# One tile for each PSUM bank in a four-layer graph network, with two-bank tiles for the ranked phases only

## The chip, the cores and the metric

The kernel runs on one core of a Trainium2 chip. The metric is the device time of one execution in microseconds; the time before is the median of three runs, 771.85 us (771.4 to 771.99). The profiled execution of the same kernel took 771.36 us, and its profile covers a span of 769.6 us, from the first to the last instruction of the program. All instants below are microseconds from the start of that span.

## What is computed

The input is a feature matrix x of 3327 nodes by 64 features and a weighted, sparse adjacency matrix of 3327 by 3327 in float32. Four graph layers follow each other, each as a residual after a layer normalisation and a ReLU:

```python
h = relu(layernorm(x));  x = x + L0(h, adj)   # two gated cells, each with its own adj product
h = relu(layernorm(x));  x = x + L1(h, adj)   # weights from the rank of each nonzero in its row
h = relu(layernorm(x));  x = x + L2(h, adj)   # three hops with w = adj * adj
h = relu(layernorm(x));  x = x + L3(h, adj)   # two hops with tanh

# L0, one cell
m  = adj @ (x @ W)
gi = m @ wih.T + bih;  gh = x @ whh.T + bhh
r  = sigmoid(i_r + h_r);  z = sigmoid(i_z + h_z)
n  = tanh(i_n + r * h_n)
out = (1 - z) * n + z * x

# L1
mask = adj != 0;  rank = cumsum(mask, axis=1);  deg = rank[:, -1:]
k = minimum(deg, 100);  pos = rank - (deg - k)
out = (mask * where(pos > 0, 0.5 ** (k - pos), 0)) @ (h @ weight) + bias
```

So eight products with a matrix of the size of adj are formed, numbered k = 0 to 7 in the kernel: 0, 1 (gated cells), 2 (ranked), 3, 4, 5 (squared), 6, 7 (plain). Everything else is small beside them.

## The kernel before

The nodes are padded to two halves of 13 blocks of 128. The result columns are split into four chunks (three of 3 blocks, one of 4), and the chunks into two groups, (0, 1) and (2, 3). A tile of adj holds 128 source nodes and the columns of one group; it is loaded from HBM into one of 19 slots on chip. For each product k and each chunk, 26 tiles are accumulated into one PSUM bank (`sums`); then the chunk's follow-up work begins. The follow-up work is a Python generator: each `yield us` says after how many microseconds of accumulating matmuls its next piece is written into the instruction streams. The engines run their own streams in order; what is written early on an engine is carried out early there.

```python
CH = [(0, 3), (3, 6), (6, 9), (9, 13)]
GROUPS = [(0, 1), (2, 3)]
STREAM_US = 0.86
...
    pairs = [psum.tile([P, 2, CWM], F32, name=f"bank{i}") for i in range(4)]
    idle_sums, idle_temps = deque(range(4)), deque(range(4, 8))
    counting = []

    def bank(i):
        return pairs[i // 2][:, i % 2]

    def take(sums=False):
        pool = idle_sums if sums or counting else idle_temps
        for c in list(tasks):
            if not pool and c not in running:
                advance(c)
        i = pool.popleft()
        return i, bank(i)

    def give(i):
        (idle_sums if i < 4 else idle_temps).append(i)
```

All eight banks are thus held as four tiles of two banks each. `take` hands out one bank, and it can lie in the same tile as another bank that is in use. Banks 0 to 3 are for the long accumulations, 4 to 7 for small products. In the ranked product (k = 2) banks 4 to 7 are used as two pairs: a running count of nonzeros is kept by matmuls with two constant matrices (`tri`, `rest`) and read by one ScalarE instruction over both banks of a pair. While `counting` holds, small products take their banks from 0 to 3.

```python
    def expand(k, c, t):                       # ranked and squared tiles
        ...
        if not counting:
            while len(idle_temps) < 4:
                advance(next(iter(tasks)))
            counting.append(True)
        a, b = GROUPS[t.g]
        pair = pairs[2 if c == a else 3]
        for s in range(2):
            if t.before is not None:
                mm(pair[:, s, :w], rest, t.before.view[:, s, t.cols(c)], start=False, unchecked=True)
            mm(pair[:, s, :w], tri, t.mask.view[:, s, t.cols(c)], start=t.before is None, unchecked=True)
        spend(STREAM_US * w / CWM)
        nc.scalar.activation(wide, pair[:, :, :w], AF.Relu, bias=bitsb, scale=-TWO7)       # L353
        ...

    def propagate(k, c, t, rhs, first, last):  # the accumulating matmuls
        ...
                nc.tensor.matmul(acc[h * D:(h + 1) * D, :w], yq, rhs[:, h, :], ...)         # L376
        ...
        spend(STREAM_US * w / CWM * (0.75 if KIND[k] == RANKED else 1.0))
        if last:
            begin(c, after[k](c, sums.pop((k, c))))

    def evacuate(acc, c):
        m = work.tile([P, CWM], F32, name="t2")[:, :width(c)]
        if c % 2:
            nc.scalar.copy(m, acc[1][:, :width(c)])                                        # L452
        else:
            nc.vector.tensor_copy(m, acc[1][:, :width(c)])                                 # L454
        give(acc[0])
        return m

    def gru(acc, c, hT, ih, hh, bi, bh, cell):
        w = width(c)
        m = evacuate(acc, c)
        yield 0.8
        ...
        for g, gate in enumerate((r, z)):
            i, ps = take()
            mm(ps[:, :w], bd[:, hh + g, :], hT, stop=False)                                # all small products: L179
            mm(ps[:, :w], bd[:, ih + g, :], m, start=False)
            nc.scalar.activation(gate, ps[:, :w], AF.Sigmoid, bias=bsum[:, cell, g:g + 1]) # L525
            give(i)
        pn = take(), take()
        for (_, ps), wt, ft in zip(pn, (hh + 2, ih + 2), (hT, m)):
            mm(ps[:, :w], bd[:, wt, :], ft)
        yield 1.0
        nc.vector.scalar_tensor_tensor(t, pn[0][1][:, :w], bcol[...], r, op0=ALU.add, op1=ALU.mult)  # L533
        nc.vector.tensor_tensor(t, t, pn[1][1][:, :w], ALU.add)                            # L534
        for i, _ in pn:
            give(i)
        nc.scalar.activation(n, t, AF.Tanh, bias=bcol[:, bi + 2:bi + 3])                   # L537
        yield 1.3
        ...                                                                                # L539 to L543: hT of the cell

    def after_hop(k):                          # the hops have the same beginning, with dense_to_nodes
        def done(c, acc):
            m = evacuate(acc, c)
            yield 0.8
            v = dense_to_nodes([(m, WL2 + k - 3)], c)
            ...
```

The order of the work: `alone` runs one product for one group, `joint` two products of one group side by side, so that each loaded tile serves both; in the last tiles of a group the order is swept chunk by chunk, so that chunk a of the group ends some tiles before chunk b.

Of the kernel before, what the change touches and what calls it, by code (L numbers as in the profile page):

```python
# [9 lines left out]
F32 = mybir.dt.float32  # L10
# [29 lines left out]
P = 128  # L40
# [6 lines left out]
CWM = 512  # L47
# [33 lines left out]
def kernel(  # L81
# [14 lines left out]
    psum = ctx.enter_context(tc.tile_pool(name="psum", bufs=1, space=bass.MemoryType.PSUM))  # L96
# [73 lines left out]
    def width(c):  # L170
        return blocks(c) * P

    def mm(out, lhsT, rhs, start=True, stop=True, unchecked=False):

        for h in range(2):
            hs = slice(h * D, (h + 1) * D)
            nc.tensor.matmul(out[hs], lhsT[:, hs], rhs, start=start, stop=stop, skip_group_check=unchecked)  # L179

    pairs = [psum.tile([P, 2, CWM], F32, name=f"bank{i}") for i in range(4)]
    idle_sums, idle_temps = deque(range(4)), deque(range(4, 8))
    counting = []

    def bank(i):
        return pairs[i // 2][:, i % 2]

    def take(sums=False):  # L190

# [9 lines that stand above are left out]
# [5 lines left out]
    def features(c):  # L206
        return feat.tile([P, width(c)], F32, name=f"hT{c}")
# [17 lines left out]
    def advance(c):  # L225
        running.add(c)
        try:
            tasks[c][1] = next(tasks[c][0])
        except StopIteration:
            del tasks[c]  # L230
        running.discard(c)
# [6 lines left out]
    def finish(c):  # L238
        while c in tasks:
            advance(c)  # L240

    def spend(us):

        for c in list(tasks):
            if c in tasks and c not in running:
                tasks[c][1] -= us
                if tasks[c][1] <= 0:
                    advance(c)
# [57 lines left out]
    def square(sq, v, turn):  # L306
        if turn % 3:
            nc.scalar.activation(sq, v, AF.Square)  # L308
        else:
            nc.vector.tensor_tensor(sq, v, v, ALU.mult)  # L310
# [16 lines left out]
    def expand(k, c, t):  # L327

        w = width(c)
        if KIND[k] == PLAIN or t.in_place:  # L330
            return t.view(c)
        wide = work.tile([P, 2, CWM], I16 if KIND[k] == RANKED else F32, name="w4", bufs=4)[:, :, :w]
        if KIND[k] == SQUARED:
            square(wide, t.view(c), t.q + c)
            return wide

        if not counting:
            while len(idle_temps) < 4:
                advance(next(iter(tasks)))
            counting.append(True)
        a, b = GROUPS[t.g]
        pair = pairs[2 if c == a else 3]
        for s in range(2):
            if t.before is not None:
                mm(pair[:, s, :w], rest, t.before.view[:, s, t.cols(c)], start=False, unchecked=True)  # L350
# [3 lines that stand above are left out]
        if c == b:  # L354
            if t.before is not None:
                t.before.free()
            if t.q == 0:
                t.mask.free()
                if t.g == 1:
                    counting.clear()  # L360
        return wide.bitcast(BF16)

    def propagate(k, c, t, rhs, first, last):
# [72 lines left out]
    def run():  # L436
        count = {}
        prepared, expanded = 0, deque()
        for i, (k, c, t) in enumerate(units):
            while prepared < len(units) and prepared < i + PREPARE[KIND[units[prepared][0]]]:  # L440
                prepare(*units[prepared])
                prepared += 1
            while len(expanded) < min(EXPAND + 1, len(units) - i):
                expanded.append(expand(*units[i + len(expanded)]))
            n = count[k, c] = count.get((k, c), 0) + 1
            propagate(k, c, t, expanded.popleft(), n == 1, n == NQ)
# [10 lines that stand above are left out]
# [57 lines left out]
# [5 lines that stand above are left out]
        rz = work.tile([P, 2, CWM], F32, name="w4", bufs=4)  # L519
        r, z = rz[:, 0, :w], rz[:, 1, :w]  # L520
        for g, gate in enumerate((r, z)):
            i, ps = take()
            mm(ps[:, :w], bd[:, hh + g, :], hT, stop=False)
# [7 lines that stand above are left out]
        nt = work.tile([P, 2, CWM], F32, name="w4", bufs=4)  # L531
        t, n = nt[:, 0, :w], nt[:, 1, :w]
        nc.vector.scalar_tensor_tensor(t, pn[0][1][:, :w], bcol[:, bh + 2:bh + 3], r, op0=ALU.add, op1=ALU.mult)  # L533
        nc.vector.tensor_tensor(t, t, pn[1][1][:, :w], ALU.add)  # L534
        for i, _ in pn:
            give(i)
        nc.scalar.activation(n, t, AF.Tanh, bias=bcol[:, bi + 2:bi + 3])  # L537
        yield 1.3
        nc.vector.tensor_tensor(r, hT, n, ALU.subtract)  # L539
        nc.vector.tensor_tensor(r, r, z, ALU.mult)  # L540
        nc.vector.tensor_tensor(r, r, n, ALU.add)
        o = features(c)
        nc.vector.tensor_scalar(o, r, 0.0, None, op0=ALU.max)  # L543
        yield 2.4
        return o
# [29 lines left out]
    def after_0(c, acc):  # L575
        hT[c] = yield from gru(acc, c, hT[c], IH1, HH1, BI1, BH1, 0)
        i, v = transpose_to_nodes(hT[c], c)
        yield 0.8
        yk = nodes(c)
        nc.vector.tensor_copy(flat(yk), v)  # L580
        give(i)
        y[1][c] = yk

    def after_1(c, acc):
        h2T = yield from gru(acc, c, hT[c], IH2, HH2, BI2, BH2, 1)
        v = transpose_to_nodes(h2T, c)
        yield 0.8
        residual(v, c)
        yk = nodes(c)
        yield from layernorm_relu(yk, c, TWO27, pace=1.5)  # L590
        add_row(c, 3)
        y[2][c] = yield from in_three(yk, c)
# [84 lines left out]
    run()  # L677
    for c in list(tasks):
        finish(c)


# [37 lines left out]
```

## Time and profile before

| what | value |
|---|---|
| median of three runs | 771.85 us |
| span of the profile | 769.6 us |
| TensorE (PE) matmuls | 721.3 us busy, 94% of the span |
| ScalarE (ACT) | 250.8 us, 33% |
| VectorE (DVE) | 235.7 us, 31% |
| adjacency tiles loaded | 286, of 768 or 896 KB, 243.55 MB with the rest of that queue |
| DMA queue of these loads | 83.3% of sixteen engines' span |
| granted TensorE clock | 1.00 throughout |

The page of the profile gives busy time and its share for each engine, the span in 40 slices, the chain of work that ended last, and groups of like instructions. The list of waits says for each engine and line how long it sat idle, and whose end released it: total, number of times, longest. PE stands for the matmuls and PEld for the weight loads that go ahead of them; one stop of the engine is listed under both. In the timeline a number in square brackets is the engine's idle time before that instruction. Where matmuls overlap in the pipeline, the profile's end of a matmul is modelled, and so "busy" is not the same as "at full rate".

### The profile page before, as it was taken

Reading aid. Unit: us, or ns where it says so; the run is one execution under the profiler, and the core shown is the slowest. Engines: PE = TensorE matmul, PEld = TensorE weight load, DVE = VectorE, ACT = ScalarE, POOL = GpSimd, SP = SyncE. Lnnn points to the kernel's source line nnn. Section 1 sums busy time; section 2 is a strip of 40 time slices with the busy share of each in tenths; the row PEclk is TensorE's granted clock in tenths of the full one; section 3 lists DMA queues with packets and bytes.
Section 4 is the critical chain, followed back from the end, with each engine's and each line's share of the span. In section 5 each row is a group of like instructions: output and inputs, shape, how many; then the busy total and the mean of one; then the engine's idle time right before and its main releaser. Section 6 shows DMA issues by size and latency. Waiting matters only on the chain.

```text
span 769.6 us, 12248 instructions
## 1 busy us (share of the span) xinstructions
PE 721.3 (94%) x5240; PEld 357.4 (46%) x5240; DVE 235.7 (31%) x346; ACT 250.8 (33%) x314; POOL 42.0 (5%) x38
## 2 busy tenths in 40 slices
PE   3977999999988999999999999999999999999997
PEld 2422433334536667776435544334344444344443
DVE  6102101215449447431944212430151510000000
ACT  1101001101036777778947421840054501000000
POOL 5000000001102001100300000000020000000000
PEclk9999999999999999999999999999999999999999
DMA  9999993669999999995999939972999199906991
GB/s 294 401 401 406 405 405 123 218 248 405 401 401 356 374 384 390 373 384 194 408 403 400 403 112 394 405 277 69 372 350 319 63 367 405 346 21 227 385 403 54
DMA packets 79174, 245.29 MB, mean 319 GB/s; under 512 B 4880, under 2 KB 5520, under 8 KB 79120
## 3 DMA queue, kind: packets, MB, share of 16 engines
q1 hardware_dynamic: 78240, 243.55, 83.3%
q10 hardware_dynamic: 880, 0.96, 0.4%
q8 instruction: 41, 0.67, 0.3%
q14 instruction: 13, 0.11, 0.0%
HBM read 243.64 MB, written 0.85 MB: 318 GB/s over the span
## 4 chain that ended last, share of the span: by engine, by line
PE 80%; DMA 9%; DVE 6%; ACT 1%; SPq 1%; issue 1%; POOL 1%; ACTq 0%; DVEq 0%; POOLq 0%
PE bank L376 64%; PE bank L179 16%; DMA adj<-in_adjT 8%; SPq L273 1%; DVE t L454 1%; DMA brow<-in_bias_rows 1%; POOL st L497 1%; ACT w L525 1%; DVE st L489 0%; DVE st L495 0%; DVE xs L505 0%; DVE t L494 0%; ACT w L353 0%; DVE y L501 0%; DVE t L491 0%
## 5 line engine op out<-in xcount | busy, mean ns | idle before, releaser
L376 PE MATMUL bank<-adj,y 128*64 128x384 f32 (+1 forms) x2704 | 492.5, 517 | 29.6 <-DMA adj<-in_adjT 19.0
L376 PEld LDWEIGHTS bank<-adj,y 128*64 128x64 f32 x2704 | 197.6, 137 | 294.5 <-issue 217.0
L353 ACT ACTIVATE w<-bank,bitsb 128x768 int16<-128x768 f32 x104 | 98.9, 953 | 31.2 <-PE bank L179 30.4
L308 ACT ACTIVATE adj<-adj 128x768 f32<-128x768 f32 (+1 forms) x103 | 85.9, 905 | 29.9 <-DMA adj<-in_adjT 25.0
L454 DVE COPY t<-bank 128x384 f32<-128x384 f32 x16 | 8.9, 557 | 280.3 <-PE bank L376 280.3
L376 PE MATMUL bank<-w,adj 128*64 128x384 bf16 (+1 forms) x624 | 73.9, 340 | 4.5 <-ACT adj L561 1.4
L179 PE MATMUL bank<-adj,tri 128*64 128x384 bf16 (+1 forms) x416 | 72.4, 339 | 0.0
L179 PE MATMUL bank<-adj,rest 128*64 128x384 bf16 (+1 forms) x400 | 70.3, 339 | 0.0
L320 DVE TENSOR_SCALAR adj<-adj 128x1536 bf16<-128x1536 f32 (+1 forms) x52 | 53.1, 1027 | 49.8 <-PE bank L179 35.9
L310 DVE TENSOR_TENSOR adj<-adj 128x768 f32<-128x768 f32 (+1 forms) x53 | 53.8, 1062 | 45.7 <-DMA adj<-in_adjT 42.4
L497 POOL TENSOR_TENSOR st<-st,mhalf 128x6 f32<-128x6 f32 (+1 forms) x16 | 27.5, 1763 | 576.8 <-DVE st L496 576.8
L525 ACT ACTIVATE w<-bank,bsum 128x384 f32<-128x384 f32 (+1 forms) x16 | 9.7, 607 | 139.0 <-PE bank L179 139.0
L376 PEld LDWEIGHTS <-adj 128*64 128x64 bf16 x624 | 40.0, 110 | 20.4 <-issue 2.3
L376 PE MATMUL bank<-w,y 128*64 128x384 f32 x208 | 36.6, 488 | 1.5 <-DVE w L310 0.8
L308 ACT ACTIVATE w<-adj 128x768 f32<-128x768 f32 x35 | 27.5, 838 | 16.8 <-PE bank L376 10.4
L452 ACT COPY t<-bank 128x384 f32<-128x384 f32 (+1 forms) x16 | 8.5, 531 | 74.1 <-PE bank L376 68.5
L179 PEld LDWEIGHTS <-tri 128*64 128x64 bf16 x416 | 26.5, 110 | 10.7 <-issue 1.2
L179 PEld LDWEIGHTS <-rest 128*64 128x64 bf16 x400 | 25.7, 110 | 9.9 <-issue 0.5
L480 ACT COPY hT<-bank 128x384 f32<-128x384 f32 (+1 forms) x12 | 6.1, 505 | 64.6 <-PE bank L179 64.6
L179 PE MATMUL bank<-bd,t 128*64 128x128 f32 (+1 forms) x320 | 26.0, 279 | 0.6 <-ACT t L452 0.4
L179 PE MATMUL bank<-hT,bd 128*64 128x384 f32 (+1 forms) x96 | 21.2, 521 | 5.7 <-ACT w L525 5.7
L310 DVE TENSOR_TENSOR w<-adj 128x768 f32<-128x768 f32 x17 | 16.0, 956 | 26.8 <-PE bank L376 20.7
(62 smaller groups left out, 263.7 us busy)
## 6 DMA issues: line engine op xcount, KB each, us to landing
adj<-in_adjT SPq DMA_DIRECT2D x156, 768.0 KB, 10.6
adj<-in_adjT SPq DMA_DIRECT2D x130, 896.0 KB, 9.6
adj<-in_weights SPq DMA_DIRECT2D x2, 352.0 KB, 7.1
xs<-in_x SPq DMA_DIRECT2D x1, 640.0 KB, 5.0
out<-xs ACTq DMA_DIRECT2D x3, 192.0 KB, 1.9
out<-xs ACTq DMA_DIRECT2D x1, 256.0 KB, 6.4
xs<-in_x SPq DMA_DIRECT2D x1, 192.0 KB, 2.4
brow<-in_bias_rows ACTq DMA_DIRECT2D x1, 96.0 KB, 6.8
```

The lines of the kernel that those rows point to most:

```text
L179: nc.tensor.matmul(out[hs], lhsT[:, hs], rhs, start=start, stop=stop, skip_group_check=unchecked)
L273: nc.sync.dma_start(out=slots[self.slot][:, :, :self.w], in_=adjT[self.q * P:(self.q + 1) * P, :].rearrange("p (s w) -> p s w", s=2)[:, :, ...
L308: nc.scalar.activation(sq, v, AF.Square)
L310: nc.vector.tensor_tensor(sq, v, v, ALU.mult)
L320: nc.vector.tensor_scalar(t.mask.view, t.view(), 0.0, None, op0=ALU.not_equal)
L353: nc.scalar.activation(wide, pair[:, :, :w], AF.Relu, bias=bitsb, scale=-TWO7)
L376: nc.tensor.matmul(acc[h * D:(h + 1) * D, :w], yq, rhs[:, h, :], start=first and n == 0, stop=last and n == len(terms) - 1)
L452: nc.scalar.copy(m, acc[1][:, :width(c)])
L454: nc.vector.tensor_copy(m, acc[1][:, :width(c)])
L480: nc.scalar.copy(ft, ps[:, :width(c)])
L497: nc.gpsimd.tensor_tensor(st[:, 3, :n], st[:, 2, :n], mhalf[:, :n], ALU.pow)
L525: nc.scalar.activation(gate, ps[:, :w], AF.Sigmoid, bias=bsum[:, cell, g:g + 1])
```

## The change

The four sum banks become four tiles of one bank. The other four banks are held in a pool of PSUM that exists twice in turn: as four tiles of one bank (`temp`), and, while the ranked product of the two groups runs, as two tiles of two banks (`pair`). `exchange` ends the one pool and opens the other at the points where the ranked product begins and ends. Its purpose is that a wait for one bank no longer covers its neighbour, while the ranked phase keeps its two-bank reads. The second part moves the writing of tanh in the gated cell: it is written one piece later, with the two `yield`s 1.0 and 0.8 in place of one of 1.3, so that ScalarE does not come to stand before tanh while its operand is still being computed. The arithmetic is the same, and so is the number of instructions that compute.

```diff
--- before.py
+++ after.py
@@ -180,12 +180,23 @@
 
 
 
-    pairs = [psum.tile([P, 2, CWM], F32, name=f"bank{i}") for i in range(4)]
     idle_sums, idle_temps = deque(range(4)), deque(range(4, 8))
+    sum_banks = [psum.tile([P, CWM], F32, name=f"sum{i}") for i in range(4)]
     counting = []
 
+    def second_half(names, shape):
+        pool = tc.tile_pool(name=names, bufs=1, space=bass.MemoryType.PSUM, reuse_waits="tile")
+        p = pool.__enter__()
+        return pool, [p.tile(shape, F32, name=f"{names}{i}") for i in range(2 if len(shape) > 2 else 4)]
+
+    half = [second_half("temp", [P, CWM])]
+
+    def exchange(names, shape):
+        half[0][0].__exit__(None, None, None)
+        half[0] = second_half(names, shape)
+
     def bank(i):
-        return pairs[i // 2][:, i % 2]
+        return sum_banks[i] if i < 4 else half[0][1][i - 4]
 
     def take(sums=False):
 
@@ -343,8 +354,9 @@
             while len(idle_temps) < 4:
                 advance(next(iter(tasks)))
             counting.append(True)
+            exchange("pair", [P, 2, CWM])
         a, b = GROUPS[t.g]
-        pair = pairs[2 if c == a else 3]
+        pair = half[0][1][c == b]
         for s in range(2):
             if t.before is not None:
                 mm(pair[:, s, :w], rest, t.before.view[:, s, t.cols(c)], start=False, unchecked=True)
@@ -358,6 +370,7 @@
                 t.mask.free()
                 if t.g == 1:
                     counting.clear()
+                    exchange("temp", [P, CWM])
         return wide.bitcast(BF16)
 
     def propagate(k, c, t, rhs, first, last):
@@ -534,8 +547,9 @@
         nc.vector.tensor_tensor(t, t, pn[1][1][:, :w], ALU.add)
         for i, _ in pn:
             give(i)
+        yield 1.0
         nc.scalar.activation(n, t, AF.Tanh, bias=bcol[:, bi + 2:bi + 3])
-        yield 1.3
+        yield 0.8
         nc.vector.tensor_tensor(r, hT, n, ALU.subtract)
         nc.vector.tensor_tensor(r, r, z, ALU.mult)
         nc.vector.tensor_tensor(r, r, n, ALU.add)
@@ -677,6 +691,7 @@
     run()
     for c in list(tasks):
         finish(c)
+    half[0][0].__exit__(None, None, None)
 
 
 # ---- launch: one core; the host only lays the arrays out ----
```

## The prediction

> **What bounds the kernel.** I read the busy times first, then the chain that ended last, then the list of waits, then the timeline around the waits. The page says that the matmul engine is the one to look at:
>
> ```profile
> PE 721.3 (94%) x5240; PEld 357.4 (46%) x5240; DVE 235.7 (31%) x346; ACT 250.8 (33%) x314; POOL 42.0 (5%) x38
> ...
> PE 80%; DMA 9%; DVE 6%; ACT 1%; SPq 1%; issue 1%; POOL 1%; ACTq 0%; DVEq 0%; POOLq 0%
> ```
>
> PE holds 80% of the chain and DMA 9%, so a stop of PE is paid in full, except in stretches where PE would only meet its next tile earlier. PE is idle for 769.6 - 721.3 = 48.3 us. The list of waits (engine and line, releaser, total us, times, longest) tells what that idle time is:
>
> ```profile
> PEld bank L376 <- DVE t L454: 18.5, 13, 2.4
> PE bank L376 <- DMA adj<-in_adjT: 19.0, 15, 12.3
> PEld bank L179 <- ACT w L525: 11.5, 8, 1.7
> PE bank L376 <- DVE t L454: 10.6, 14, 1.8
> PE bank L179 <- ACT w L525: 5.7, 8, 0.8
> ACT w L537 <- DVE w L534: 20.2, 8, 2.9
> ```
>
> The DMA line is mostly the start (12.3 us in one wait). The two lines that matter are the 14 waits of an accumulating matmul (L376) for L454, and the 8 waits of a gate matmul (L179) for L525. L454 copies a finished sum of chunk a out of its bank; the matmul that waits belongs to chunk b and writes another bank, the other half of the same two-bank tile. Nothing in the arithmetic asks for it. The timeline at one such place:
>
> ```profile
> 445.52 3.07 PE L376 MATMUL bank<-adj,y 128*64 128x384 f32 x17
> 448.62 0.56 DVE L454 COPY t<-bank 128x384 f32<-128x384 f32 x1 [5.00 <-PE bank L376]
> 449.24 1.51 PE L376 MATMUL bank<-adj,y 128*64 128x384 f32 x8 [0.65 <-DVE t L454]
> 450.58 0.82 PE L179 MATMUL bank<-bd,t 128*64 128x128 f32 x12
> ```
>
> PE ends at 448.59, DVE copies from 448.62 to 449.18, PE goes on at 449.24. The gates show the same form: z (or the pair after it) is to be written while r (or z) is being read by the sigmoid in the other half of the tile:
>
> ```profile
> 217.39 0.58 ACT L525 ACTIVATE w<-bank,bsum 128x384 f32<-128x384 f32 x1 [0.65 <-PE bank L179]
> 218.02 0.20 PEld L179 LDWEIGHTS bank<-hT,bd 128*64 128x64 f32 x4 [1.35 <-ACT w L525]
> 218.02 0.87 PE L179 MATMUL bank<-hT,bd 128*64 128x384 f32 x4 [0.68 <-ACT w L525]
> ```
>
> **What the Trainium skill says.** "PSUM — Partial Sum Buffer", section "PSUM bank collisions raise a hardware error", asks for guarding by bank (and quarter of the partitions), and states that two engines on different banks run clean; so the removed waits guard nothing. The trace already has such overlaps: at 612.94 ScalarE copies a sum (L452, 0.48 us) while PE accumulates in another tile. "Perfetto Trace Analysis", section "Matmuls", says that independent groups should rotate through banks so that the copy of one overlaps the matmuls of the next. The kernel rotates, but in 14 of 32 copies the overlap is lost. The same page, section "Tensor Engine Instruction (MATMUL, LD_WEIGHTS)", warns that a matmul's end is an estimate; here the copies begin 0.03 us after the shown end, so it is nearly right, but it tells me to cost a stop from start to start and not by the shown gap.
>
> **The cost of one stop.** Matmuls of 384 columns follow each other every 0.16 us when nothing stops them, though each lasts 0.517 us by the page; they overlap. So the shown gap of 0.66 us leaves out the overlap that is lost. I took the starts of the four matmuls before and the eight after each stop and subtracted the time that their columns need at the steady pace. A stop for L454 costs 0.89 to 0.97 us (one of them 2.04), a stop for L525 0.92 (1.02 and 1.08 for 512 columns). In sum 14.0 us for L454 and 7.6 us for L525. Two more false waits stand in the ranked product, where small products live beside the sums: the one at 230.7 (for L505) costs 0.27 and the one at 233.2 (for L534) 0.42. All that can be removed is 14.0 + 7.6 + 0.7 = 22.3 us.
>
> **The change part by part.** The instruction lists of both kernels hold the same work (4782 instructions on PE, 348 on DVE) in nearly the same order; some tiles only change slots. With one-bank tiles the accumulating matmuls no longer wait for L454 anywhere; the wait for that copy now stands on the first matmul that reads the copied sum. The waits for the sigmoid stay only where the same bank comes round again, long after it was read. The tri matmuls at the start of the ranked product wait for a sigmoid and for L534, as they did for L533 and L534 before, so the exchange of pools adds no new stop that I can find. What each removal is worth depends on the stretch:
>
> ```profile
> core 0: us, PE busy (x) PEld busy (x) DVE busy (x) ACT busy (x) POOL busy (x), PEclk, DMA share, GB/s
> ...
> 62.00:124.00 62.00, 59.58 (x340) 23.80 (x342) 8.09 (x15) 3.92 (x7) 0.00 (x0) 1.00 0.98 388
> 124.00:168.00 44.00, 40.53 (x238) 16.02 (x236) 10.40 (x18) 5.62 (x9) 0.00 (x0) 1.00 0.50 180
> 168.00:220.00 52.00, 48.31 (x298) 22.38 (x296) 26.42 (x43) 6.72 (x11) 5.96 (x4) 1.00 0.99 383
> 220.00:250.00 30.00, 25.61 (x276) 16.70 (x272) 22.39 (x40) 18.93 (x26) 5.52 (x4) 1.00 0.99 372
> 250.00:357.00 107.00, 106.15 (x1200) 76.76 (x1202) 48.28 (x57) 81.79 (x87) 5.70 (x4) 1.00 0.95 357
> ...
> 380.00:770.00 390.00, 377.53 (x2472) 172.06 (x2468) 87.64 (x117) 106.15 (x141) 6.77 (x4) 1.00 0.77 290
> ```
>
> (The columns are busy time and number of instructions of PE, PEld, DVE, ACT and POOL, then clock, DMA share, GB/s.)
>
> - 62 to 124: the DMA engines are full (0.98). Stops at 63.9, 68.7 and 75.0 cost 0.95 + 0.92 + 0.92 = 2.8 us. The tile with the least room landed at 121.29 and was first used at 124.01, so PE can gain at most 2.7 us here. Worth **2.7**.
> - 124 to 168: DMA is half idle and its loads wait for slots that PE frees. Stops at 125.5, 129.8, 138.8, 161.6, 165.9: 0.90 + 0.92 + 1.02 + 0.90 + 0.92 = **4.7**. The loads that run without a pause afterwards begin with a slot freed at 168.3, so they begin about 7.4 us earlier as well.
> - 168 to 250: DMA is full (0.99), and DVE's masks for the ranked product wait for landings (13.8 us by the waits of L320). Stops at 178.0, 213.3, 218.0, 227.2 and the two small ones: 1.08 + 2.04 + 0.92 + 0.92 + 0.69 = 5.65. At 213 the copy stood behind a mask that waited for its tile, so part of that moves to the gate matmul that needs the copy; at 250.4 PE waits 1.4 us for features of the next layer, whose DVE chain does not shorten by as much. I choose half: **2.8**.
> - 250 to 380: no such stops; PE is 106.15 of 107 us busy in the steady part. Worth 0, but earlier gains pass through.
> - 380 to the end: ten stops for L454 at 400.4, 449.2, 473.4, 523.7, 553.1, 606.3, 632.3, 685.3, 717.9 and 758.4: 0.96 + 0.92 + 0.90 + 0.90 + 0.90 + 0.89 + 0.90 + 0.96 + 0.97 + 0.90 = **9.2**. The least room of a tile is 9.1 us in the full-DMA stretch up to 447 and 2.8 at the very end, against one stop inside each; so they count in full.
> - New waits: the copied sum is ready about 1.15 us after the start of the chunk's last matmul (same timeline). The product that reads it follows 0.16 us plus two units of 0.645 later, 1.45, where the next chunk is 384 wide: no stop. Where it is 512 wide only one unit of 0.86 is between, 1.02: a stop of 0.13, some five times. With a DVE square of 1 us in the way now and then I put **-1.0** for all.
> - tanh: moving it takes ACT's waits for L534 (20.2 us) off a stream that is 33% busy, and lengthens the cell's chain by half a microsecond of written work. ACT ends almost no wait of PE outside the sigmoids. Worth 0.
>
> Sum: 2.7 + 4.7 + 2.8 + 0 + 9.2 - 1.0 = 18.4; 771.85 - 18.4 = **753.4 us**.
>
> **Rivals.**
> - *The waits only move.* The copy is still needed, and if the product reading it comes too soon PE stops there instead. For it: the 0.13 us above, and DVE squares of about 1 us. Against it: the 16 ScalarE copies (L452) have been in this position all along and cost PE 0.4 us in all by the list of waits. At worst half of the 14 stops remain: about 760 us.
> - *DMA takes the gain.* The page has the loads at 83.3% of the span, so at 753 they would be at 85%; slack shrinks only inside full stretches. If all of 62 to 250 were bound by loads, 2.7 + 9.2 - 1.0 remain: 761 us.
> - *The ranked start passes on more.* If DVE and DMA follow PE fully between 168 and 250, another 2.85 us come: about 750.5.
> - *The later tanh or the new pool puts a new stop into the start of the ranked product*, where DVE, ACT and PE hang on each other within a few microseconds. It could eat the 2.8 us and a little more: 757.
>
> **Range and chances.** The 9.2 + 4.7 us are nearly certain; the unsure parts are the 2.8 (between -1 and +5.6), the early 2.7 (if the tile that lands at 121.29 holds PE longer), and -1.0 (down to -4). That gives 749.5 to 757.5 as eight in ten. The 2% line is at 756.4, 3.0 us above the estimate, hence 0.77 for faster by over 2%, 0.22 for within, 0.01 for slower.
>
> **What would show it.** In the profile after: the accumulating matmul has no line waiting for the DVE copy, the gate matmuls lose nearly all of their 5.7 us for the sigmoid, a small new wait of gate and dense matmuls for the DVE copy appears (under 2 us), PE's busy share rises above 95%, ACT's waits for L534 shrink. The ranked steady part begins about 10 us earlier than 250, and its end keeps that distance. What would prove me wrong: PE's waits for landings in the first 250 us growing by more than 3 us, or PE waiting at the first ranked tiles.

## The result and the profile after

The changed kernel takes **753.59 us** (751.8 to 754.2, four runs) against 771.76 us; the ratio is 0.9761 with a 95% interval of 0.9743 to 0.9779. The prediction was 753.4 us. The profiled execution took 751.8 us with a span of 750.1, that is 19.5 us less than the 769.6 of before. The medians differ by only 18.2 us because three of the four runs after had a granted TensorE clock of 0.995 to 0.998, and 753.2 to 754.2 us; the profiled one had 1.00.

The page after, busy times and chain:

```profile
PE 717.0 (96%) x5240; PEld 345.7 (46%) x5240; DVE 235.7 (31%) x346; ACT 250.6 (33%) x314; POOL 42.0 (6%) x38
...
PE 83%; DMA 8%; DVE 5%; SPq 1%; issue 1%; POOL 1%; ACT 1%; ACTq 0%; DVEq 0%; POOLq 0%
```

DVE and ACT do what they did before; PE's idle time fell from 48.3 to 750.1 - 717.0 = 33.1 us, 15.2 less. Its busy time fell by 4.3 us for the same 5240 matmuls. That fits the stops: each costs about 0.9 us from start to start and shows 0.66 us as idle, so part of its cost is booked as busy time. Together that is the 19.5 us. The list of waits after (engine and line, releaser, total, times, longest; line numbers have moved, L389 accumulates, L467 and L465 copy a sum, L538 is the sigmoid, L547 and L551 are the second sum and tanh of the n gate):

```profile
PE sum L389 <- DMA adj<-in_adjT: 19.7, 16, 12.4
...
ACT w L551 <- DVE w L547: 6.0, 4, 1.8
...
PEld temp L179 <- DVE t L467: 4.6, 7, 2.0
```

There is no line of an accumulating matmul waiting for the copy and none of a gate matmul waiting for the sigmoid. Waiting for landings is as before (19.0, now 19.7). tanh's wait fell from 20.2 to 6.0 us; the one-bank tiles alone bring it to 13.8 (the kernel of the first experiment). The place that the prediction showed at 445.52 now looks like this in the timeline (weight loads left out):

```profile
433.65 4.68 PE L389 MATMUL sum<-adj,y 128*64 128x384 f32 x28
437.10 0.56 DVE L467 COPY t<-sum 128x384 f32<-128x384 f32 x1 [3.97 <-PE sum L389]
438.17 0.82 PE L179 MATMUL temp<-bd,t 128*64 128x128 f32 x12
```

The copy lies beside the accumulating matmuls, and the product that reads it (438.17) starts without a stop.

For the time between, I set the start of the same matmul in both traces against each other. The gain so far, in us, with the kernel of the first experiment (tanh back) beside it; "again" is a second execution of each, from a later session:

| where, in the time of before | predicted | after | after, again | tanh back | tanh back, again |
|---|---|---|---|---|---|
| 115 (full DMA) | 2.7 | 1.88 | 1.28 | 2.75 | 2.32 |
| 168.3, first load of the full stretch | 7.4 | 5.6 | 5.0 | 7.3 | 6.9 |
| 253, steady ranked part | 10.2 | 10.41 | 10.01 | 11.50 | 10.49 |
| 370 | 10.2 | 10.52 | 10.12 | 11.61 | 10.60 |
| last matmul | 18.4 | 19.56 | 19.17 | 20.68 | 19.67 |

Two executions of one kernel thus differ by up to 1.0 us at one place, all four at a clock of 1.00; the second ones are 0.4 to 0.6 us behind the first already at 60 us.

### The profile page after: what moved, and what is told of

The parts are those of the page before. It is cut to its first block, busy times and chain, and to the rows that moved or that the text cites. A ratio compares the mean times of both kernels' runs of the same rounds, so it can differ in the third digit from the quotient of the medians.

```text
span 750.1 us, 12253 instructions
## 1 busy us (share of the span) xinstructions
PE 717.0 (96%) x5240; PEld 345.7 (46%) x5240; DVE 235.7 (31%) x346; ACT 250.6 (33%) x314; POOL 42.0 (6%) x38
## 4 chain that ended last, share of the span: by engine, by line
PE 83%; DMA 8%; DVE 5%; SPq 1%; issue 1%; POOL 1%; ACT 1%; ACTq 0%; DVEq 0%; POOLq 0%
PE sum L389 66%; PE pair L179 9%; PE temp L179 8%; DMA adj<-in_adjT 7%; SPq L284 1%; PE sum L179 1%; DMA brow<-in_bias_rows 1%; DVE adj L331 1%; POOL st L510 1%; DVE t L504 1%; DVE st L502 0%; DVE xs L518 0%; DVE adj L321 0%; DVE st L508 0%; DVE t L507 0%
## 5 line engine op out<-in xcount | busy, mean ns | idle before, releaser
L389 PE MATMUL sum<-adj,y 128*64 128x384 f32 (+1 forms) x2704 | 489.8, 516 | 21.7 <-DMA adj<-in_adjT 19.7
L389 PEld LDWEIGHTS sum<-adj,y 128*64 128x64 f32 x2704 | 192.4, 137 | 289.9 <-issue 249.1
L365 ACT ACTIVATE w<-pair,bitsb 128x768 int16<-128x768 f32 x104 | 98.8, 954 | 33.1 <-PE pair L179 30.1
L467 DVE COPY t<-sum 128x384 f32<-128x384 f32 x16 | 8.9, 558 | 275.0 <-PE sum L389 275.0
L389 PE MATMUL sum<-w,adj 128*64 128x384 bf16 (+1 forms) x624 | 72.9, 340 | 3.4 <-ACT adj L575 2.2
L179 PE MATMUL pair<-adj,tri 128*64 128x384 bf16 (+1 forms) x416 | 70.8, 339 | 0.0
L179 PE MATMUL pair<-adj,rest 128*64 128x384 bf16 (+1 forms) x400 | 68.7, 339 | 0.6 <-ACT w L365 0.4
L331 DVE TENSOR_SCALAR adj<-adj 128x1536 bf16<-128x1536 f32 (+1 forms) x52 | 53.1, 1028 | 51.2 <-PE pair L179 38.6
L538 ACT ACTIVATE w<-temp,bsum 128x384 f32<-128x384 f32 (+1 forms) x14 | 8.6, 611 | 138.8 <-PE temp L179 138.8
L389 PEld LDWEIGHTS <-adj 128*64 128x64 bf16 x624 | 36.8, 110 | 22.0 <-ACT adj L575 2.8
L389 PE MATMUL sum<-w,y 128*64 128x384 f32 x208 | 36.4, 487 | 0.8 <-DVE w L321 0.8
L465 ACT COPY t<-sum 128x384 f32<-128x384 f32 (+1 forms) x16 | 8.5, 532 | 71.9 <-PE sum L389 71.9
L179 PE MATMUL temp<-bd,t 128*64 128x128 f32 (+1 forms) x296 | 24.3, 279 | 0.4 <-ACT t L465 0.4
L321 DVE TENSOR_TENSOR w<-adj 128x768 f32<-128x768 f32 x17 | 16.0, 956 | 25.9 <-PE sum L389 19.7
L389 PEld LDWEIGHTS sum<-w,y 128*64 128x64 f32 x208 | 14.5, 137 | 18.7 <-issue 14.8
```

Of the source, the lines that this page charges most:

```text
L331: nc.vector.tensor_scalar(t.mask.view, t.view(), 0.0, None, op0=ALU.not_equal)
```

## The experiments

Theory: the gain is the false waits removed, 0.9 us each, less what landings hide. Rivals: the waits only move; the two kinds of wait hide each other; tanh carries part of it. Ratios are to the kernel before, run on the same chip in the same session; in the three sessions that kernel had medians of 771.8, 772.2 and 773.5 us.

**tanh back.** In the changed kernel:

```diff
-        yield 1.0
         nc.scalar.activation(n, t, AF.Tanh, bias=bcol[:, bi + 2:bi + 3])
-        yield 0.8
+        yield 1.3
```

> The changed kernel with tanh written where it was before. Theory (the gain is the removed false waits alone; tanh is worth nothing): 753.6 us, within 1.0 of the changed kernel. Rival (moving tanh carries part of the gain, because ScalarE no longer stands before it): 756 us or more, with the wait of tanh for the second sum of the n gate back at some 20 us.

Measured: 751.0 us (750.65 to 751.59), ratio 0.9723 (0.9706 to 0.9740). Neither: without the tanh move the kernel is faster, so the move costs time and the one-bank tiles alone bring more than the whole change. To see whether that was chance, both were run again on one chip, together with the move in one cell only (`if cell == 1:` or `if cell == 0:` around the early `yield`).

> The changed kernel once more, to stand beside the next three on the same chip: 751.8 to 754.2 us.

> The changed kernel with tanh where it was, again, beside the changed kernel on one chip. Theory (the later tanh costs time: the first cell's result comes one piece later, and the first matmul on it stops for its copy at about 81 and 142 us in the changed kernel, 0.9 us each; some of it is won back in the second cell): 1 to 2.5 us less than the changed kernel. Rival (the difference of the first run of it came from the chip and the clock): within 0.5 us of it.

> tanh moved in the second cell only. Theory (the cost sits in the first cell, in the two stops for the copy of its result; in the second cell the move neither costs nor gains more than 1 us): no stops for that copy, 0.9 us each, and 750 to 751.5 us, like the kernel with tanh back in both cells. Rival (the cost sits in the second cell, at the start of the ranked product, where the next layer's features come later): like the changed kernel, 752.5 us or more.

> tanh moved in the first cell only. Theory (the cost sits in the first cell): the two stops for the copy are there, and the time is that of the changed kernel or up to 1.5 us over it, 752.5 to 754.5 us. Rival (second cell): like the kernel with tanh back, 750 to 751.5 us.

| tanh moved in | us, lowest to highest | ratio, interval |
|---|---|---|
| both cells | 752.99, 751.6 to 754.09 | 0.9749, 0.9730 to 0.9768 |
| none | 751.05, 750.81 to 751.65 | 0.9726, 0.9711 to 0.9741 |
| second cell | 752.21, 750.82 to 752.56 | 0.9735, 0.9718 to 0.9751 |
| first cell | 752.99, 752.33 to 756.01 | 0.9758, 0.9736 to 0.9779 |

The direction of the first run repeated (2.6, then 1.9 us), while the intervals of the two kernels overlap this time. At a clock of 1.00 the difference is about 0.8 us (751.6 to 752.2 against 750.65 to 751.65), and by the two pairs of profiles 1.1 and 0.5. The rest goes with clocks of 0.995 to 0.998, which five of the eight runs with tanh moved had and none of the eight with tanh back. It was not tested whether the move brings these clocks about; the kernel before has such clocks too. The first cell's share can be read in the timeline. First the changed kernel, then the one with tanh back (weight loads left out):

```profile
79.56 0.82 PE L179 MATMUL temp<-ident,hT 128*64 128x128 f32 x12
80.44 0.56 DVE L594 COPY y<-temp 128x384 f32<-128x384 f32 x1 [1.86 <-PE temp L179]
81.05 1.72 PE L389 MATMUL sum<-adj,y 128*64 128x384 f32 x8 [0.66 <-DVE y L594]
```

```profile
78.07 0.82 PE L179 MATMUL temp<-ident,hT 128*64 128x128 f32 x12
78.73 1.67 PE L389 MATMUL sum<-adj,y 128*64 128x384 f32 x8
78.94 0.56 DVE L593 COPY y<-temp 128x384 f32<-128x384 f32 x1 [1.64 <-PE temp L179]
```

With tanh moved, the cell's result is written so late that the first matmul of the next product stands directly behind its transposition and must wait for the copy. With tanh back, matmuls that do not need it stand between. The stop comes at 81 and again at 142 us, 0.9 us each from start to start. Of these four kernels it is there in the two that move tanh in the first cell, and not in the other two.

In the second cell the move shifts stops. With tanh back (again), PE stops three times between 220 and 228 us (0.72, 1.07 and 0.98 us) and at 240 us once, for 1.44 us, for the split of the next layer's features into three terms. With tanh moved in the second cell only, the three are gone, PE stops for 0.44 us at 233 us, and at 238 and 239 us for the split (1.18 and 0.98 us). At this point that execution is 0.8 us ahead of tanh back, again (11.31 us gained against 10.49). Then the granted clock of PE falls to half for 3.41 us (columns as in the prediction; the clock is the third from the end):

```profile
239.85:243.26 3.41, 3.41 (x24) 2.03 (x22) 2.47 (x3) 0.90 (x1) 0.00 (x0) 0.50 1.03 401
243.26:247.00 3.74, 3.74 (x50) 2.59 (x46) 0.21 (x1) 2.70 (x3) 0.00 (x0) 1.00 0.99 363
```

That takes 1.68 us, and 9.63 are left at 253. So the 752.2 us of this kernel, between its two ranges, do not decide between theory and rival: four of its five runs had a clock of 0.996 or 0.998, and the one at 1.00 took 751.72. The first cell's part is shown: two stops, 1.5 to 1.9 us behind tanh back by 150 us; 0.5 to 1.1 us are left at 253. What the move does in the second cell, 0.8 us for the better in this one trace, is no larger than the difference between two executions of one kernel, and stays open.

**One part of the change at a time.** Sums alone in one-bank tiles, the small products in two fixed tiles of two banks:

```diff
-    pairs = [psum.tile([P, 2, CWM], F32, name=f"bank{i}") for i in range(4)]
+    sum_banks = [psum.tile([P, CWM], F32, name=f"sum{i}") for i in range(4)]
+    pairs = [None, None] + [psum.tile([P, 2, CWM], F32, name=f"bank{i}") for i in (2, 3)]
```

and small products alone, the sums in pairs beside the exchanged pool:

```diff
-    sum_banks = [psum.tile([P, CWM], F32, name=f"sum{i}") for i in range(4)]
+    sum_pairs = [psum.tile([P, 2, CWM], F32, name=f"sum{i}") for i in range(2)]
```

Both were first run with tanh moved, then with tanh back.

> Only the four sums get one-bank tiles; the four small-product banks stay two fixed tiles of two banks (tanh as in the changed kernel). Theory: the stops at the copies of finished sums go, the eight stops at the sigmoids stay at 0.9 us each and partly count: 759 us (757.5 to 761). Rival (waits only move, or the ranked start passes on the gain by itself): within 1.5 us of the changed kernel, 752 to 755, or over 764.

> Only the small products get one-bank tiles, exchanged for two pairs in the ranked product; the sums stay in two tiles of two banks. Theory: six of the eight sigmoid stops go, fourteen stops at copies of sums stay (most now at the ScalarE copies, because the pairing comes out otherwise): 766.5 us (764 to 768.5), and the gains of this run and of the sums-only run add up to the 18.3 us of the whole change within 2.5. Rival (the two parts overlap, since one stop hides the other): their gains add up to 22 or more.

> One-bank tiles for the sums alone, with tanh where it was before: one part of the change without the other. Theory: the ten stops after 380 us are gone, worth 9 us, and the three sum stops before 168 us (2.75 us) shift the start of the loads; the sigmoid stops stay. 758.3 us (757 to 760).

> One-bank tiles for the small products alone, exchanged for pairs in the ranked product, with tanh where it was before. Theory: five sigmoid stops before 168 us (1.84 + 2.86 us) and the one at 178 are gone, worth 4 to 6 us; of those after 200 us little counts, because the copy at about 210 us stands behind masks whose tiles have not landed and still stops PE. All stops for sums after 380 us are there. 767 us (765.5 to 769), and this gain and that of the sums alone add up to the gain of both together (20.8 us with tanh back) within 3 us. Rival (the later tanh, not the landings, made the run with tanh moved gain only 2.0 us): 764 or less.

| one-bank tiles for | tanh | us, lowest to highest | ratio, interval |
|---|---|---|---|
| sums | moved | 759.78, 758.17 to 763.12 | 0.9829, 0.9806 to 0.9851 |
| small products | moved | 769.74, 767.72 to 773.64 | 0.9971, 0.9958 to 0.9983 |
| sums | back | 757.8, 756.85 to 758.45 | 0.9797, 0.9774 to 0.9820 |
| small products | back | 768.95, 765.2 to 769.46 | 0.9932, 0.9908 to 0.9956 |

With tanh back, the two parts bring 773.47 - 757.8 = 15.7 and 773.47 - 768.95 = 4.5 us, together 20.2; both at once brought 771.8 - 751.0 = 20.8 and 21.1 in the two runs. The fastest runs of each, which leave out most of the differences of the clock, give 14.2 + 5.9 = 20.1 against 20.3 and 20.1. They add up, so neither hides the other. With tanh moved they bring 12.0 and 2.1, short of the 18.2 of the whole by 4.1 us where 2.5 were allowed, and the small-product run missed its range by 1.2 us. How much of this is the later tanh and how much the clock is not separated: all eighteen runs of the small-product kernel had a clock of 0.991 to 0.997, and the one run of the sums kernel at 1.00 took 758.17 us, which lies within the range with tanh back.

Why the small products bring so little is seen in the timeline of that kernel with tanh back, around the copy of chunk 0 in product 1:

```profile
206.32 0.96 DVE L331 TENSOR_SCALAR adj<-adj 128x1536 bf16<-128x1536 f32 x1 [1.03 <-DMA adj<-in_adjT]
208.25 0.96 DVE L331 TENSOR_SCALAR adj<-adj 128x1536 bf16<-128x1536 f32 x1 [0.97 <-DMA adj<-in_adjT]
209.13 0.55 DVE L467 COPY t<-sum 128x384 f32<-128x384 f32 x1
209.73 1.96 PE L389 MATMUL sum<-adj,y 128*64 128x384 f32 x8 [4.06 <-DVE t L467]
```

The copy comes in VectorE's stream behind masks (L331) that each wait for a tile to land. PE had gained 5.8 us on the kernel before by 188 us. There the same copy stops PE for 1.78 us:

```profile
213.25 1.51 PE L376 MATMUL bank<-adj,y 128*64 128x384 f32 x8 [1.78 <-DVE t L454]
```

Here it is 4.06, so 3.5 us of the gain are left after it. From 210.66 us the clock of this execution was 0.50 for 3.41 us, which took another 1.7, and at 253 us 2.7 are left. (The one run of this kernel at a clock of 1.00 took 765.2 us, the four at 0.996 to 0.998 took 768.5 to 769.5.) A false wait on a stream that waits for DMA passes that DMA wait on to PE.

**The dose raised.** All four sums in one tile:

```diff
-    sum_banks = [psum.tile([P, CWM], F32, name=f"sum{i}") for i in range(4)]
+    sum_quad = psum.tile([P, 4, CWM], F32, name="sums")
```

> The dose raised: all four sums in one tile of four banks, small products as in the changed kernel. Now an accumulating matmul waits for the copy at 29 of the 32 finished sums, against none in the changed kernel and 14 in the sums-paired run. Theory (each such wait stops PE for about 0.9 us and is paid in full outside full-DMA stretches): the sums-paired time plus 15 times 0.9, some 779 us (776 to 782). Rival (the waits only move to the product that reads the copy): within 3 us of the sums-paired run, 770 or less.

Measured: 781.38 us (780.09 to 784.29), ratio 1.0121 (1.0091 to 1.0150). The waits of its accumulating matmuls for the two copies:

```profile
PE sums L389 <- DVE t L467: 12.2, 14, 3.1
...
PE sums L389 <- ACT t L465: 8.7, 13, 1.1
```

Against the sums-paired run beside it (10 and 4 such stops) 13 stops more cost 11.6 us, 0.9 each. (27 such stops came where 29 were expected. Two stops of small products in the ranked product, 0.7 us of idle time each, also came with the one tile; counted in, it is 0.8 for each.) The waits do not move: they are paid.

**Beyond both kernels.** From the kernel with tanh back, two steps against what is left at the start of the ranked product: first ScalarE copies chunk 0's sum in product 1, then also the pieces up to the split into three terms are written closer together.

```diff
-        if c % 2:
+        if c % 2 or act:               # act: cell == 1 and c == 0
             nc.scalar.copy(m, acc[1][:, :width(c)])
```

```diff
-        yield from layernorm_relu(yk, c, TWO27, pace=1.5)
+        yield from layernorm_relu(yk, c, TWO27, pace=1.0)
 ...                                    # in_three, both places
-            yield 0.8
+            yield 0.4
```

> The kernel with tanh back, and the finished sum of chunk 0 in product 1 copied by ScalarE in place of VectorE, whose stream stands there before masks that wait for landings. Theory (that order of work on VectorE holds PE at 206 us for 1.1 to 1.65 us, and the loads allow PE to run ahead): the stop goes and 0.5 to 1.7 us of it count, 749.5 to 750.5 us. Rival (the landings bound the start of the ranked product whichever engine copies): within 0.4 us of the kernel with tanh back, 750.7 to 751.5.

> The ScalarE copy, and the pieces between the second cell and the split of its features into three terms written closer together, so that the features PE waits for at about 239 us (1.1 us in the kernel with tanh back) are there earlier. Theory (the order in which the pieces are written bounds that chain): the stop shrinks below 0.5 us and the time is 0.5 to 1.5 us below the ScalarE-copy kernel, 748.5 to 749.8 us. Rival (the chain is bound by VectorE's masks behind landings): no change against that kernel, or a new stop of the pair matmuls for ScalarE.

The ScalarE copy gave 751.67 us (751.17 to 754.18), ratio 0.9722 (0.9700 to 0.9745): no gain over tanh back, whose ratio is 0.9723, though the time is 0.2 us outside the range of the rival. The stop for the copy is gone, and the same masks now hold the next VectorE instruction of the cell (L546), for which the first tri matmul waits:

```profile
210.27 0.96 DVE L331 TENSOR_SCALAR adj<-adj 128x1536 bf16<-128x1536 f32 x1 [1.01 <-DMA adj<-in_adjT]
211.15 0.61 DVE L546 SCALAR_TENSOR_TENSOR w<-temp,bcol,w 128x384 f32<-128x384 f32 x1
211.81 0.83 PE L179 MATMUL pair<-adj,tri 128*64 128x384 bf16 x4 [2.20 <-DVE w L546]
```

(The profiled execution is the slowest of the six, its landings here are about 1 to 2 us later than with tanh back, and its clock was 0.50 for 3.41 us from 211.88 us; the median stands for the kernel.) This speaks for the rival: whichever engine copies, VectorE's part of the cell stands behind masks that wait for landings. Whether an order of VectorE's work with L546 ahead of the masks would help was not tried. Closer pieces made it slower, 755.13 us (753.66 to 757.81), ratio 0.9765 (0.9741 to 0.9789):

```profile
236.98 0.51 ACT L574 CAST adj<-y 128x384 bf16<-128x384 f32 x1 [3.68 <-DVE y L514]
237.40 0.89 ACT L365 ACTIVATE w<-pair,bitsb 128x768 int16<-128x768 f32 x1
238.32 0.51 ACT L574 CAST adj<-y 128x384 bf16<-128x384 f32 x1
238.34 0.53 PE L179 MATMUL pair<-adj,rest 128*64 128x384 bf16 x2 [3.28 <-ACT w L365]
```

ScalarE stands 3.68 us before a cast whose operand is not there yet, with the reading of the next pair (L365) behind it, and PE stands 3.28 us before that pair, the new stop that the rival named. In the same execution the clock was 0.50 for 6.83 us from 237.34 us, and all five runs had clocks of 0.995 to 0.997, so stop and clock share the 3.5 us over the ScalarE copy; how much is each was not separated. The best of all versions is the changed kernel with tanh where it was: 751.0 us.

## Why the prediction was right, point by point

- **What bounds the kernel, and the cost of a stop.** Right. The ten stops after 380 us were put at 9.2 us; the gain grows from 10.52 at 370 to 19.56 at the end, 9.04. The dose run gives 0.8 to 0.9 for each.
- **Equal work.** Right, though the prediction's counts (4782 on PE, 348 on DVE) are not those of the profile, which has 5240 matmuls on PE and 346 instructions on DVE in both kernels.
- **62 to 124 us.** Put at 2.7, came out as 1.88; with tanh back it is 2.75. The step that failed is "tanh: worth 0": the later tanh made the stop at 81 us.
- **124 to 168 us.** The first load of the full stretch was to start 7.4 us earlier. It starts at 162.77 in place of 168.34, 5.6 earlier; with tanh back at 161.02, 7.3. Again tanh, by the stop at 142 us and the later pieces of the cell.
- **168 to 250 us.** I chose half of 5.65, so 2.8. From 5.6 at the loads to 10.41 the changed kernel gained 4.8; with tanh back from 7.3 to 11.50, 4.2; in the second executions it was 5.0 and 3.6. That half was mis-sized by 0.8 to 2.2 us. Its reason was right: the landings do hold this part, as the masks before the copy show in the small-products run and before L546 in the ScalarE copy run. Why more than half came through was not tested.
- **New waits, -1.0.** Not there after 380 us: the products after a 512-column unit, for which I put 0.13 us, show no new stop over 0.25 us. There is one, of 1.30 us, for the copy at 207 us, the very place that the 168-to-250 step named.
- **The sum.** 18.4 against a gain of 19.5 in the profiles and 18.2 in the medians. The hit within 0.2 us is partly luck. At a clock of 1.00 the kernel takes 751.8 us, 1.6 under the prediction. In its profile three errors partly cancel: the part up to the loads brought 1.8 us less (the later tanh), the ranked start 2.0 more, and the part after 380 us 0.8 more, since the new waits did not come. Three of the four runs had lower clocks and took 1.4 to 2.4 us more than that, which the prediction did not foresee, and this put the median at 753.59.

## What to carry to other kernels

A wait follows the tile, not the bank: where one tile spans two PSUM banks, a copy from one bank stops matmuls into the other, and with PE the bound each such stop costs about 0.9 us, of which the profile's idle column shows 0.66. Measure a stop from start to start, and then ask per stretch whether loads would take the gain. Do not ship a second edit with the first unmeasured: the piece moved "for free" cost about 1 us at full clock, and 1.9 to 2.6 by the medians, of the 20.8 us that the first part brings alone, because in-order engines turn a later-written piece into a wait of whatever needs it next.

## What was unexpected

PE's granted clock differs between executions of one kernel (0.995 to 1.00 in the four runs of the changed kernel), and its time with it by about 2 us (751.8 at 1.00, 754.2 at 0.995), as much as some of the effects studied here. The traces show what such a mean is made of: seven of the fourteen profiles have stretches of 3.41 or 6.83 us, nine in all, at a clock of 0.50, between 60 us and the last microseconds of the program, and 1.00 around them. While PE is busy, such a stretch takes half its length, 1.7 or 3.4 us. Each of the nine begins within about 1 us of the end of a stop of PE (0.66 to 4.06 us long); but many like stops are followed by none, and why was not tried. So before a difference of a microsecond or two is put down to an edit, the clock of both traces in that stretch has to be looked up.
